# A graph-attention and adjacency kernel: the row of q by way of DRAM and one spreading load, with new order lists

## The chip, the cores and the metric

The kernel runs on one core of one Trainium2 chip. The metric is device time in microseconds (us): the median of several runs, beside one execution that the hardware profiler recorded. The engines are TensorE (PE in the profile, PEld for its weight loads), VectorE (DVE), ScalarE (ACT), GpSimd (POOL) and SyncE (SP), which only issues DMAs here.

## The reference

There are 32 batches x[b] of 512 channels by 1024 nodes, a matrix adj of 512 by 512, vectors wq, wk and bm of 512 and a bias of 1024. All is f32.

```
q, k   = wq . x, wk . x                                # one number per node
scores = leaky(q[n] + k[m], slope 0.01)                # 1024 x 1024
att    = softmax(scores over n)
agg    = x att^T;  gnn0 = relu(adj agg + bm)
x      = layernorm(x + gnn0, over the 1024 nodes)      # layer 0
x      = layernorm(x + (adj * adj)^T x + bias)         # layer 1, adj * adj elementwise
```

## The kernel before

The attention of layer 0 is never made as a matrix. exp(leaky(q + k)) is one product of exponentials where q + k > 0 and another where it is not, so if the nodes are sorted by q, the sum over n for a node m is a prefix sum plus a suffix sum at a place that depends on k[m]. A batch passes through these steps; the short name is the one that the order lists use:

- `ld` loads x[b] in four pieces of 0.5 MB (L87). `pa` (parts, L221) multiplies with wq and wk into one PSUM bank, the nodes in four groups of 256, group g at partition 32g (q) and 32g + 1 (k). `pc` (L229) copies that to SBUF on ScalarE, `co` (L236) transposes it, and `cc` (L241) copies q and k to `qkc`: node j*128 + p at partition p, column j.
- `ro` (row, L252) makes the row of q on all partitions: eight transposes of a column of q broadcast to 128, into a PSUM tile of 1024 floats. `rc` (row_copy, L261) copies it on VectorE to `qb` and takes its maximum in the same instruction; two small instructions make -max and -0.01 max (L262, L263).
- `rk` (L271, eight times, VectorE) counts for 128 nodes how many q are larger: their rank. `ct` (L284, eight times, ScalarE, a Sign with a sum) counts the same for -k. `re`, `oq` and `ce` turn these into indices and set bounds; `we` takes exponentials.
- `z` (product, L310, eight times) is adj times x for 128 nodes, 3.43 us of TensorE each; `zc` (L316, ScalarE) copies it to the one buffer `zt`. `sc` (scatter, L324, GpSimd, indirect DMA) writes the rows of zt to DRAM in the order of rank.
- `sl` loads the sorted rows to the one buffer `tab`, eight consecutive rows to a partition (L343), `se` takes exponentials (L348, L349), `u` and `d` (L362, L372, VectorE) sum along a partition upward and downward, `cu`, `cd` (L380, TensorE) and `uc`, `dc` (L387, ScalarE) carry over partitions, and `tu`, `te`, `td` (L405, L414) add the carries.
- `tw` and `tl` write the table of sums to DRAM (L422, 2 MB twice, and L425, one row). `g` (L432, eight indirect DMAs on GpSimd) gathers its rows into the one buffer `got`. `mw`, `ms`, `mx` (L445 to L459) mix the two halves, and `t` (turn, L482) transposes the mix.
- `r`, `s0`, `rt`, `rce`, `n0` (L490 to L508) add it to x and normalize: layer 0 is done.
- Layer 1 is one level of Strassen-Winograd on quarters: `t1` to `t4` (VectorE, L519 to L533) form differences; t1 overwrites a quarter of x, t2 has a tile of its own, t3 and t4 lie in zt. `U`, `V`, `Y`, `Z`, `11`, `12`, `21` (L540, L575, 1.7 us of TensorE each, twice) multiply, and U and Z begin with a small matmul for the bias (L538). `Uc`, `Vc`, `Zc`, `up`, `lr`, `ll`, `ls` take the results, `s1`, `r1`, `n` (L468, L475, L631) normalize, and `st` writes the output (L636).

TensorE sees in the steady state the end of layer 1 of one batch, four z of the next, transposes of the mix, parts and cols of the one after, and four more z.

The order on every engine is written out by hand: under a manual schedule each instruction is issued where it stands in the lists `head`, `loop` and `tail`, whose words are an operation, a batch (relative to the loop's in `loop`, to the last in `tail`) and an index. The program is laid out for every engine in this one order, and an engine takes its own instructions strictly in order; a wait therefore holds all that stands behind it on that engine. SP's DMAs are on one queue. Buffers are reused by tag; a tile waits for the readers of the one before it in that buffer. In the loop the words of interest stand thus (others left out):

```
t.-3.1 r.-3.1 pa.0 t.-3.0 pc.0 co.0 st.-4.2 z.-1.4 cc.0 z.-1.5 n.-4.3 st.-4.3 cd.-2 z.-1.6 dc.-2 td.-2.0
td.-3.1 ro.-1 tw.-3.0 z.-2.7 tw.-3.1 tl.-3 t1.-4 rc.-1 U.-4.0 rk.-1.7 U.-4.1 rk.-1.5 ct.-1.3 rk.-1.0 11.-4.1
```

(the second line is the start of the next turn of the loop, where batches are counted one lower).

Of the kernel before, what the change touches and what calls it, by code (L numbers as in the profile page):

```python
# [49 lines left out]
def adj_resnorm_kernel(  # L50
# [48 lines left out]
    nbm = const.tile([P, CT], F32, name="nbm")  # L99
# [21 lines left out]
    eps = const.tile([P, 1], F32, name="eps")  # L121
    nc.vector.memset(eps, EPS)
    power = const.tile([P, CT], F32, name="power")
# [12 lines left out]
    zero = one.tile([P, ZR], F32, tag="carry", name="zero")[0:1, :]  # L136
    nc.vector.memset(zero, 0.0)
    sorted_z = [dr.tile([N, ZR], F32, name=f"sorted_z_{i}") for i in range(2)]
# [3 lines left out]
    spare = const.tile([1, 1], F32, name="spare")  # L142
# [7 lines left out]
    first_0 = const.tile([6, P], BF16, name="first_0")  # L150
    first_10 = const.tile([6, P], BF16, name="first_10")
# [25 lines left out]
    def bias_parts(b):  # L177


        own = const.tile([6, 8], F32, name="own")  # L180
# [4 lines left out]
        nc.vector.tensor_copy(first_0, own[:, 4:5].broadcast_to([6, P]))  # L185
        nc.vector.memset(first_10, 1.0)
        rest, done = room[:, 0, :], room[:, 1, :]
        for i in range(3):
            part = one.tile([P, N], BF16, tag="junk_s", name=f"bias_part_{i}")[0:6, 0:H]
            nc.vector.tensor_copy(part, rest)  # L190
            if i < 2:
                nc.vector.tensor_tensor(rest, rest, part, ALU.subtract)
            if i == 0:
                nc.vector.tensor_scalar(done, part, own[:, 0:1], None, ALU.mult)
            else:
                nc.vector.scalar_tensor_tensor(
                    done, part, own[:, i : i + 1], done, ALU.mult, ALU.add
                )
# [27 lines left out]
    def parts_copy(b):  # L226
        s = st[b]
        s.part = one.tile([P, Q], F32, tag="part", name=f"part_{b}")
# [9 lines left out]
    def cols_copy(b):  # L238
        s = st[b]
        s.qk = s4.tile([P, NT, 2], F32, tag="qk", name=f"qkc_{b}")  # L240
# [5 lines left out]

    def row(b):

        s = st[b]
        s.ps = p2.tile([P, N], F32, tag="w", name=f"q_tp_{b}")  # L250
        for j in range(NT):
            nc.tensor.transpose(  # L252
                s.ps[:, j * P : (j + 1) * P], s.qk[:, j, 0:1].broadcast_to([P, P]), ident
            )

    def row_copy(b):
        s = st[b]
        s.qb = one.tile([P, N], F32, tag="qb", name=f"qb_{b}")
        top = s4.tile([P, 3], F32, tag="top", name=f"top_{b}")
        s.top, s.ntop = top[:, 0:1], top[:, 1:3]  # L260
        nc.vector.tensor_scalar(s.qb, s.ps, 1.0, None, ALU.mult, ALU.max, accum_out=s.top)  # L261
# [19 lines left out]
    def count(b, j):  # L281
        s = st[b]
        junk = one.tile([P, N], BF16, tag="junk_s", name=f"junk_s_{b}_{j}")
# [114 lines left out]
    def carry_down_copy(b):  # L398
        st[b].carry = one.tile([P, ZR], F32, tag="carry", name=f"carry_{b}")
# [62 lines left out]
    def stats(b, name):  # L462
        return [sp.tile([P, CT], F32, tag=t + name, name=f"{t}{name}_{b}") for t in ("tot", "var")]

    def spread(b, i, t, v, name):

        junk = one.tile([P, N], BF16, tag="junk_s", name=f"junk_{name}_{b}_{i}")
# [30 lines left out]
    def root0(b):  # L498
            v = st[b].v0
            nc.scalar.activation(v[1], v[1], AF.Sqrt, scale=1.0 / N**3, bias=eps)  # L500

    def root0_end(b):
            v = st[b].v0
            nc.vector.reciprocal(v[1], v[1])  # L504
    
# [39 lines left out]
    def rows1(b, m):  # L545
        s = st[b]
        if not s.v1:
            s.v1 = stats(b, "1")
            s.nb = sp.tile([P, CT], F32, tag="nb", name=f"nb_{b}")
            s.part2 = sp.tile([P, CT], F32, tag="part2", name=f"part2_{b}")  # L550
# [84 lines left out]
    def store(b, m):  # L635
# [7 lines left out]
        "rc": row_copy, "rk": rank, "re": rank_end, "ct": count, "ce": count_end,  # L643
# [21 lines left out]
    bias.0 ld.1 ld.2 ld.3 pa.0 z.0.0 pc.0 co.0 zc.0.0 z.0.1 cc.0 ro.0 zc.0.1 pa.1 rc.0 ct.0.1  # L665
    rk.0.1 z.0.2 ct.0.3 rk.0.7 pc.1 rk.0.2 ct.0.5 z.0.4 rk.0.3 ct.0.2 rk.0.4 ct.0.7 rk.0.6 z.0.6
    zc.0.4 zc.0.2 rk.0.0 rk.0.5 co.1 zc.0.6 z.0.5 re.0 cc.1 ct.0.4 oq.0 sc.0.1 sc.0.6 z.0.3
    sc.0.0 zc.0.5 ct.0.6 sc.0.5 sc.0.2 z.0.7 zc.0.3 sc.0.4 ct.0.0 sc.0.3 ro.1 zc.0.7 sc.0.7
    z.1.0 rc.1 rk.1.3 ct.1.6 ct.1.5 rk.1.1 z.1.6 sl.0.0 sl.0.1 rk.1.7 rk.1.5 z.1.2 zc.1.6 rk.1.6
    ct.1.4 rk.1.0 zc.1.0 se.0.0 oq.1 rk.1.2 z.1.4 se.0.1 u.0.0 ct.1.1 ce.0 u.0.1 u.0.2 z.1.1  # L670
    rk.1.4 u.0.3 u.0.4 z.1.5 u.0.5 zc.1.1 zc.1.4 u.0.6 ct.1.3 u.0.7 zc.1.2 ct.1.7 d.0.7 pa.3
    d.0.6 zc.1.5 re.1 d.0.5 sc.1.1 cu.0 pc.3 d.0.4 ct.1.2 sc.1.5 co.3 z.1.3 d.0.3 uc.0 sc.1.2
    cc.3 d.0.2 ct.1.0 tu.0.0 sc.1.0 sc.1.4 z.1.7 d.0.1 zc.1.3 te.0 sc.1.3 d.0.0 tl.0 tu.0.1
    sc.1.6 cd.0 ro.3 dc.0 zc.1.7 pa.2 td.0.0 sc.1.7 z.2.5 rc.3 tw.0.0 rk.3.0 ct.3.0 ct.3.6
    td.0.1 z.2.0 zc.2.5 ct.3.3 ce.1 tw.0.1 rk.3.6 pc.2 ct.3.1 co.2 z.2.4 rk.3.3 ct.3.2 rk.3.1
    ct.3.4 rk.3.4 ct.3.5 z.2.3 cc.2 rk.3.7 zc.2.0 ct.3.7 rk.3.5 g.0.0 sl.1.0 zc.2.4 sl.1.1 ro.2
    rk.3.2 g.0.3 z.2.6 rc.2 g.0.1 ct.2.4 rk.2.2 zc.2.3 z.2.7 rk.2.6 ct.2.0 rk.2.1 we.0 se.1.0
    ct.2.3 rk.2.5 z.2.1 g.0.2 u.1.0 ce.3 g.0.4 u.1.1 oq.2 u.1.2 g.0.6 se.1.1 zc.2.6 rk.2.0 z.2.2
    zc.2.7 g.0.5 ct.2.7 rk.2.3 g.0.7 mw.0.0 rk.2.4 z.3.0 ms.0.2 ms.0.1 mx.0.2 ms.0.0 rk.2.7
    zc.2.1 ms.0.3 ct.2.1 u.1.3 z.3.4 re.2 mx.0.0 sc.2.6 ct.2.2 mw.0.1 sc.2.5 mx.0.1 ms.0.6  # L680
# [282 lines left out]
```

## Time and profile before

| what | value |
|---|---|
| median of 3 runs | 2062.61 us (2061.65 to 2064.26) |
| the profiled execution's own time | 2065.32 us |
| its span, first to last instruction | 2063.6 us |
| mean granted TensorE clock | 0.991 |
| DMA traffic | 541.04 MB, 262 GB/s over the span |
| DMA busy share, SP's queue / GpSimd's queue | 41.2% / 26.0% of 16 engines |
| GpSimd busy | 874.6 us (42%) |

The page of a profile gives, for each engine, its busy time and share of the span. A group's line names the line of the code, the engine, the operation, output<-input by tile name, the shapes and the count; after the bar stand its busy time and the mean duration of one instruction in ns, and after a second bar the idle time of the engine just before such instructions, with what ended it. A stretch's line has its bounds and length, then busy time and count of each engine (PE, PEld, DVE, ACT, POOL), the granted clock, the share of time that the 16 DMA engines were busy, and GB/s. A line of the timeline has start, duration, engine, line, operation and how many were merged. A line of waits has the waiting engine with its tile and line, the releaser, the sum of the idle time, how often, and the longest.

### The profile page before, as it was taken

The numbers are of one execution on the slowest core, as the hardware profiler recorded it, in microseconds if no ns is written. First come the engines' busy times: TensorE is split into PE (matmuls) and PEld (weight loads), VectorE is DVE, ScalarE is ACT, GpSimd is POOL, SyncE is SP. The second block draws the span as 40 slices with busy tenths as digits, with TensorE's granted clock in tenths as the row PEclk, the third lists the DMA queues.
The fourth block names the chain that finished last, engine by engine and source line by source line (L and its number), as shares of the span: only waits on it lengthen the run. The fifth ranks groups of instructions, "written<-read, shape, count | busy, mean of one in ns | idle before, by whom it ended". The sixth has DMA issues, their size and how long they took to land. (4 is left out here: it accounts for less than half of the span.)

```text
span 2063.6 us, 22066 instructions
## 1 busy us (share of the span) xinstructions
PE 2004.7 (97%) x6609; PEld 956.7 (46%) x6609; DVE 1674.9 (81%) x2778; ACT 1496.3 (73%) x2560; POOL 874.6 (42%) x1106
## 2 busy tenths in 40 slices
PE   8999999999999999999999999999999999999976
PEld 4444444444444444444444544444444444444432
DVE  6888898798877889887889888789778888789672
ACT  3566787678776777777777777777777777767566
POOL 4344543344343444443444443453444443443421
PEclk9999999999999999999999999999999999999988
DMA  5558776866667766667766767766677766677752
GB/s 226 212 222 312 275 287 266 306 264 257 271 245 291 307 255 246 271 266 292 306 241 250 273 268 296 290 249 258 255 276 306 276 244 268 245 269 273 286 204 82
DMA packets 137967, 541.04 MB, mean 262 GB/s; under 512 B 14404, under 2 KB 14416, under 8 KB 129656
## 3 DMA queue, kind: packets, MB, share of 16 engines
q1 hardware_dynamic: 80464, 337.47, 41.2%
q0 software_dynamic: 57344, 202.15, 26.0%
q8 instruction: 52, 0.85, 0.2%
q14 instruction: 67, 0.55, 0.1%
q10 hardware_dynamic: 40, 0.02, 0.0%
HBM read 270.29 MB, written 269.29 MB: 261 GB/s over the span
## 5 line engine op out<-in xcount | busy, mean ns | idle before, releaser
L310 PE MATMUL z_ps<-adj_t,x 128*128 128x512 f32 x2048 | 906.6, 593 | 0.4 <-ACT zt L316 0.4
L310 PEld LDWEIGHTS z_ps<-adj_t,x 128*128 128x128 f32 x2048 | 384.1, 190 | 448.0 <-issue 439.5
L324 POOL DMA_INDIRECT sorted_z<-zt,to x256 | 377.2, 1473 | 481.0 <-ACT zt L316 403.7
L432 POOL DMA_INDIRECT got<-table,of x256 | 262.2, 1024 | 209.6 <-issue 87.8
L271 DVE SCALAR_TENSOR_TENSOR junk_v<-qb,qkc,tie 128x1024 uint8<-128x1024 f32 x256 | 328.2, 1282 | 4.0
L284 ACT ACTIVATE junk_s<-qb,qkc 128x1024 bf16<-128x1024 f32 x256 | 293.9, 1148 | 18.9 <-DVE qb L261 17.0
L475 POOL TENSOR_SCALAR var<-var 128x1 f32<-128x1 f32 x128 | 46.3, 362 | 461.9 <-ACT junk L468 458.6
L454 ACT ACTIVATE got<-got,w 128x512 f32<-128x512 f32 x256 | 172.2, 713 | 64.2 <-DVE w L449 56.6
L316 ACT COPY zt<-z_ps 128x512 f32<-128x512 f32 x256 | 144.4, 577 | 68.4 <-PE z_ps L310 63.2
L459 DVE SCALAR_TENSOR_TENSOR got<-got,w 128x512 f32<-128x512 f32 x256 | 180.9, 745 | 10.9 <-ACT got L454 10.7
L490 DVE SCALAR_TENSOR_TENSOR x<-agg_ps,nbm,x 128x1024 f32<-128x1024 f32 x128 | 161.4, 1280 | 23.1 <-PE agg_ps L482 22.7
L372 DVE SCALAR_TENSOR_TENSOR tab<-tab,ac 128x513 f32<-128x513 f32 x224 | 168.0, 750 | 3.0
L631 ACT ACTIVATE g<-g,nb,var 128x1024 f32<-128x1024 f32 x128 | 157.8, 1238 | 11.8 <-POOL nb L625 11.8
L468 ACT ACTIVATE junk<-g,tot 128x1024 bf16<-128x1024 f32 x128 | 146.6, 1146 | 21.3 <-DVE g L595 16.8
L362 DVE SCALAR_TENSOR_TENSOR tab<-tab,ac 128x514 f32<-128x514 f32 x192 | 144.5, 752 | 16.9 <-ACT ac L348 11.7
L468 ACT ACTIVATE junk<-x,tot 128x1024 bf16<-128x1024 f32 x128 | 146.8, 1147 | 13.6 <-DVE x L490 8.3
L405 DVE TENSOR_TENSOR tab<-tab,carry 128x2052 f32<-128x2052 f32 x64 | 144.8, 2292 | 11.5 <-ACT carry L387 11.5
L540 PE MATMUL sum_ps<-x,adj 128*128 128x512 f32 x256 | 131.4, 637 | 16.3 <-ACT x L508 16.3
L482 PE MATMUL agg_ps<-ident,got 128*128 128x128 f32 x1024 | 133.4, 278 | 11.2 <-issue 4.7
L508 ACT ACTIVATE x<-x,var 128x1024 f32<-128x1024 f32 x128 | 138.5, 1149 | 0.7 <-DVE var L504 0.6
L601 DVE SCALAR_TENSOR_TENSOR g<-sum_ps,g 128x512 f32<-128x512 f32 x64 | 44.0, 687 | 111.8 <-ACT junk_s L284 75.3
L482 PEld LDWEIGHTS agg_ps<-ident,got 128*128 128x128 f32 x1024 | 115.2, 143 | 36.3 <-DVE x L490 12.2
(121 smaller groups left out, 2698.8 us busy)
## 6 DMA issues: line engine op xcount, KB each, us to landing
table<-tab SPq DMA_DIRECT2D x64, 2056.0 KB
tab<-sorted_z SPq DMA_DIRECT2D x64, 1028.0 KB
x<-in_x_dram SPq DMA_DIRECT2D x128, 512.0 KB
out_dram<-g SPq DMA_DIRECT2D x128, 512.0 KB
sorted_z<-zt,to POOLq DMA_INDIRECT x256
got<-table,of POOLq DMA_INDIRECT x256
adj_in<-in_adj_dram SPq DMA_DIRECT2D x1, 1024.0 KB
table<-end SPq DMA_DIRECT2D x32, 2.0 KB
```

The lines of the kernel that those rows point to most:

```text
L271: nc.vector.scalar_tensor_tensor(junk, s.qb, s.q[:, j : j + 1], tie[:, at : at + N], ALU.subtract, ALU.is_gt, accum_out=s.rank[:, j : j + 1],)
L284: nc.scalar.activation(junk, s.qb, AF.Sign, bias=s.k[:, j : j + 1], accum_out=s.sign[:, j : j + 1])
L310: nc.tensor.matmul(s.z[j], xt[:, c, j * P : (j + 1) * P], adj_t[:, c, :], start=(c == 0), stop=(c == CT - 1),)
L324: nc.gpsimd.indirect_dma_start(out=sorted_z[b % 2][:, :], out_offset=bass.IndirectOffsetOnAxis(ap=s.to[:, j : j + 1], axis=0), in_=zt[:, j ...
L372: nc.vector.scalar_tensor_tensor(v, v, c, s.zs[:, j + 1, 0:D], ALU.mult, ALU.add)
L432: nc.gpsimd.indirect_dma_start(out=s.got[:, j, :], out_offset=None, in_=table[b % 2][:, :], in_offset=bass.IndirectOffsetOnAxis(ap=s.of[:, ...
L454: nc.scalar.activation(down, down, AF.Copy, scale=s.w[:, 1, j : j + 1])
L459: nc.vector.scalar_tensor_tensor(up, up, s.w[:, 0, j : j + 1], down, ALU.mult, ALU.add)
L468: nc.scalar.activation(junk, t, AF.Square, bias=v[0][:, i : i + 1], scale=-float(N), accum_out=v[1][:, i : i + 1],)
L482: nc.tensor.transpose(s.agg[o][:, j * P : (j + 1) * P], s.got[:, j, o * P : (o + 1) * P], ident)
L490: nc.vector.scalar_tensor_tensor(t[:, o, :], s.agg[o], nbm[:, o : o + 1], t[:, o, :], ALU.max, ALU.add, accum_out=s.v0[0][:, o : o + 1],)
L631: nc.scalar.activation(g, g, AF.Identity, bias=s.nb[:, m : m + 1], scale=s.v1[1][:, m : m + 1])
```

## The change

The row of q no longer passes through TensorE. `pc` copies the parts to SBUF as before; a new step `qw` (row_out) writes the q partitions (0, 32, 64, 96) of `part` as a row of 1024 floats to DRAM, and `ro` is now one DMA on SP that loads this row to all 128 partitions of `qb`. `rc` (row_max) only takes the maximum. There are two buffers of qb instead of one. To find room, `part`, the downward carry and T2 share one buffer, ScalarE's unused results ("junk_s") are written in 8 bits instead of 16, qkc has three buffers instead of four, the two bias selectors are one column each and broadcast, and several small tiles are put together. All three order lists are new, with qw after pc and with rc later than before; their description says that they were laid out for 5 per cent longer work on the engines beside TensorE. The loop now covers batches 13 to B - 6 instead of 12 to B - 7.

```diff
-    first_0 = const.tile([6, P], BF16, name="first_0")
-    first_10 = const.tile([6, P], BF16, name="first_10")
+    first = const.tile([6, 16], BF16, name="first")
+    first_0, first_10 = first[:, 0:1].broadcast_to([6, P]), first[:, 1:2].broadcast_to([6, P])
...
     def parts_copy(b):
         s = st[b]
-        s.part = one.tile([P, Q], F32, tag="part", name=f"part_{b}")
+        s.part = one.tile([P, 2, H], F32, tag="T2", name=f"part_{b}")[:, 0, 0:Q]
         nc.scalar.copy(s.part, s.ps)
...
-        s.qk = s4.tile([P, NT, 2], F32, tag="qk", name=f"qkc_{b}")
+        s.qk = s3.tile([P, NT, 2], F32, tag="qk", name=f"qkc_{b}")
...
+    def row_out(b):
+        rows = q_row[b % 2].rearrange("(g o c) -> g o c", g=CT, o=1)
+        nc.sync.dma_start(
+            out=rows, in_=st[b].part.rearrange("(g r) c -> g r c", g=CT)[:, 0:1, :]
+        )
+
     def row(b):
 
         s = st[b]
-        s.ps = p2.tile([P, N], F32, tag="w", name=f"q_tp_{b}")
-        for j in range(NT):
-            nc.tensor.transpose(
-                s.ps[:, j * P : (j + 1) * P], s.qk[:, j, 0:1].broadcast_to([P, P]), ident
-            )
-
-    def row_copy(b):
-        s = st[b]
-        s.qb = one.tile([P, N], F32, tag="qb", name=f"qb_{b}")
+        s.qb = sp.tile([P, N], F32, tag="qb", name=f"qb_{b}")
+        nc.sync.dma_start(out=s.qb, in_=q_row[b % 2].partition_broadcast(P))
+
+    def row_max(b):
+        s = st[b]
         top = s4.tile([P, 3], F32, tag="top", name=f"top_{b}")
         s.top, s.ntop = top[:, 0:1], top[:, 1:3]
-        nc.vector.tensor_scalar(s.qb, s.ps, 1.0, None, ALU.mult, ALU.max, accum_out=s.top)
+        nc.vector.tensor_reduce(s.top, s.qb, axis=AX.X, op=ALU.max)
...
-        junk = one.tile([P, N], BF16, tag="junk_s", name=f"junk_s_{b}_{j}")
+        junk = one.tile([P, N], U8, tag="junk_s", name=f"junk_s_{b}_{j}")
...
-        st[b].carry = one.tile([P, ZR], F32, tag="carry", name=f"carry_{b}")
+        st[b].carry = one.tile([P, 2, H], F32, tag="T2", name=f"carry_{b}").rearrange("p i c -> p (i c)")[:, 0:ZR]
...
-        return [sp.tile([P, CT], F32, tag=t + name, name=f"{t}{name}_{b}") for t in ("tot", "var")]
+        t = sp.tile([P, 2, CT], F32, tag="tv" + name, name=f"tv{name}_{b}")
+        return [t[:, 0, :], t[:, 1, :]]
...
-        junk = one.tile([P, N], BF16, tag="junk_s", name=f"junk_{name}_{b}_{i}")
+        junk = one.tile([P, N], U8, tag="junk_s", name=f"junk_{name}_{b}_{i}")
...
-    for b in range(12, B - 6):
+    for b in range(13, B - 5):
```

The new loop list, from the transposes of the mix to the first products of layer 1, and the start of the head:

```
t.-3.1 uc.-2 n.-4.0 t.-3.3 r.-3.1 s1.-4.3 pa.0 st.-4.0 d.-2.3 s0.-3.1 r.-3.3 r1.-4.3 t.-3.0 pc.0 d.-2.2 s0.-3.3 qw.0
t.-3.2 d.-2.1 co.0 n.-4.2 sc.-1.2 z.-1.4 r.-3.2 st.-4.2 sc.-1.3 r.-3.0 st.-4.1 s0.-3.2 cc.0 s0.-3.0 d.-2.0 z.-1.5
tu.-2.0 zc.-1.4 rt.-3 sc.-1.4 te.-2 tu.-2.1 n.-4.3 cd.-2 st.-4.3 z.-1.7 ro.0 dc.-2 rce.-3 tl.-2 zc.-1.5 td.-2.0 n0.-3.0
sc.-1.5 n0.-3.2 td.-2.1 z.-1.6 tw.-2.0 n0.-3.1 n0.-3.3 rc.0 tw.-2.1 U.-3.0 rk.0.5 ct.0.4 zc.-1.6 rk.0.2 U.-3.1 ct.0.1
rk.0.0 11.-3.1 Uc.-3.1 t1.-3 Uc.-3.0 zc.-1.7 rk.0.7 ct.0.5 11.-3.0 sc.-1.7 t2.-3 ct.0.2 sc.-1.6 Z.-3.0 rk.0.1 g.-2.0
...
ld.1 bias.0 pa.0 z.0.0 pc.0 qw.0 ro.0 pa.1 ld.2 zc.0.0 co.0 z.0.5 cc.0 pc.1 qw.1 rc.0 ct.0.7 rk.0.3
```

## The prediction

> **What bounds the kernel now.** I read the page's busy line first, then busy time by stretch, then TensorE's own waits, and last the timeline of one batch in the middle.
>
> ```profile
> PE 2004.7 (97%) x6609; PEld 956.7 (46%) x6609; DVE 1674.9 (81%) x2778; ACT 1496.3 (73%) x2560; POOL 874.6 (42%) x1106
> ```
>
> TensorE (PE) is at work in all but 58.9 us of the span. Where that idle time lies is shown by the busy time of five stretches:
>
> ```profile
> 7.00:100.00 93.00, 91.37 (x363) 44.44 (x364) 72.52 (x121) 45.91 (x86) 37.52 (x48) 1.00 0.55 212
> 100.00:300.00 200.00, 192.97 (x611) 91.41 (x610) 172.86 (x290) 143.23 (x255) 94.38 (x111) 0.99 0.73 278
> 300.00:1900.00 1600.00, 1593.24 (x5287) 761.23 (x5286) 1331.23 (x2210) 1200.37 (x2054) 693.28 (x867) 1.00 0.70 272
> 1900.00:2063.60 163.60, 127.08 (x352) 59.53 (x350) 95.65 (x153) 105.47 (x169) 45.98 (x72) 0.90 0.47 181
> ```
>
> The first pair of numbers is length and PE busy time. From 300 to 1900 us PE is idle 6.8 us of 1600; the gaps are in the fill (7.0 us before the first matmul, 8.7 us up to 300) and in the drain (36.5 us). So in the middle a batch costs what PE needs for it, and the drain is a chain of latencies. TensorE's waits between 60 and 1900 us, in all 12.9 us, are short ones for neighbours:
>
> ```profile
> PE agg_ps L482 <- DVE got L459: 4.5, 9, 1.0
> PE qk_tp L236 <- ACT part L229: 4.0, 3, 3.2
> ```
>
> The work that goes is the group "q_tp", and the timeline shows what it occupies:
>
> ```profile
> L252 PE MATMUL q_tp<-ident,qkc 128*128 128x128 f32 x256 | 33.3, 273 | 0.5 <-DVE qkc L241 0.5
> ...
> 990.48 3.59 PE L310 MATMUL z_ps<-adj_t,x 128*128 128x512 f32 x8
> 993.91 1.04 PE L252 MATMUL q_tp<-ident,qkc 128*128 128x128 f32 x8
> 994.78 3.60 PE L310 MATMUL z_ps<-adj_t,x 128*128 128x512 f32 x8
> 998.31 0.39 PE L538 MATMUL sum_ps<-bias_p,first 6*128 6x512 bf16 x1
> ```
>
> The product after it starts 0.87 us after the transposes start, not 1.04: the ends overlap. The next q_tp starts at 1055.91, so a batch takes 62.0 us.
>
> **What the Trainium skill says.** (1) "Perfetto Trace Analysis", Identifying the Most-Contended Engine: matmul busy time misleads, since matmuls are pipelined. The trace agrees: the group's 33.3 us of busy time is only 32 slots of 0.87 to 0.88 us. (2) "DMA: Bandwidth & Descriptors", Two DMAs through the same engine are not ordered: a DMA that reads what another wrote must be held at its issuing engine until the first one's semaphore is full. So the row load stands on SP until the row write has landed; the kernel before has the same with its sorted rows. (3) The same page, Anatomy of one DMA, puts about 2 us of fixed cost on each DMA. Here it is more: in the drain half a load of sorted rows (1 MB) was issued at 1937.24 and used at 1942.89, 5.6 us, of which 2.5 us are bytes at the 421 GB/s that the fullest 5 us moved; 3.1 us stay. (4) "VectorE: DVE Perf Modes", the perf-mode tier table: tensor_reduce has only the 1x rate. No large one is in this trace.
>
> **The change, part by part.**
>
> *Transposes removed.* 32 slots of 0.88 us are 28.2 us; the waits for "qkc" ahead of them were 0.5 us more. All lie where PE never rests or before the last product (about 1931 us), on which the drain hangs, so the whole 28.7 us leave the path. Bounds: 27.8 (0.87 each) to 33.3 (the group's busy time).
>
> *VectorE.* The fused copy from PSUM (1219 ns and 83 to read the sum) becomes a reduction of 1024 floats in SBUF. An estimate from the page's 1x rate at 0.96 GHz is 1.07 us and a start; the 1024-wide tensor-tensor rows take 1.22 us. I take 1.22, bounds 1.07 to 1.35. It is hidden: VectorE is idle about 10 us of each 62. Uncovered, the upper bound would cost 0.05 us a batch, 1.6 us in all.
>
> *Two DMAs a batch on SP.* The row write is small and on few partitions; the nearest row, "table<-end", keeps SP 1.11 us. The row load is 128 rows of 4 KB, 0.5 MB, 0.35 us of SP. The traffic per batch goes from 16.9 to 17.4 MB. Where the load goes the engines are half free:
>
> ```profile
> 1049.00:1051.00 2.00, 2.00 (x6) 0.95 (x5) 2.00 (x3) 2.00 (x4) 1.74 (x3) 1.00 0.20 80
> 1051.00:1053.00 2.00, 2.00 (x8) 1.23 (x7) 1.19 (x2) 1.97 (x4) 1.99 (x2) 1.00 0.63 240
> 1053.00:1055.00 2.00, 2.00 (x6) 0.86 (x5) 1.64 (x2) 2.00 (x5) 0.85 (x1) 1.00 0.56 218
> 1055.00:1057.00 2.00, 2.00 (x12) 1.39 (x11) 2.00 (x2) 2.00 (x3) 1.64 (x2) 1.00 0.31 132
> ```
>
> (the last two columns are DMA share and GB/s). The question is whether the row lands in time. Count from the first agg transpose of the batch, T (1038.91 in the trace). In the new loop list SP has, in order, qw, three stores, ro, tl, tw. The write waits for the copy of qk_ps, about T+3, and lands by T+9 even at the 4.85 us that a loaded "table<-end" took. The last store waits for n.-4.3, whose place among ScalarE's work is nearly the old one (T+12.4), so ro is issued at T+13.1. With 5.6 us, as above (half the bytes, but one 0.5 MB store just ahead), the row is there at T+18.7. VectorE, going through the same r, d, tu and td steps, is free at T+19.7 (T+19.0 in the trace plus one d moved behind T, 0.7). Then rc 1.4, three ranks 4.0 and T1 1.22 end at T+26.3. PE needs T1 at Z: agg transposes, parts and cols 5.6, four z 13.7, cd 0.9, two U 4.5, two C11 3.4, thus T+28.3. So 2 us of room, and the row may land as late as T+21.7, 8.6 us after issue, before PE feels it. On ScalarE count, zc, sc and then the gathers queue behind the row: at T+18.7 plus 5 us of ACT work the scatters go at T+24 and the gathers at T+27, where the old ones began at T+31.5. tl and tw stand behind ro on SP, but tw waits for td until T+17 anyway; 0.5 MB ahead of it is 1.2 us of the 4.5 us thus won. Cost taken: nothing; bounds 0 to 3 us a batch (below).
>
> *Sharing of buffers.* part and carry now lie in T2's buffer. The carry copy waits for qw, landed at T+9 against cd at T+13; part waits for V of the batch before, 20 us earlier. Cost 0; if the write were 4 us later, ScalarE would stand and td with it. A second qb buffer lets the load start while the old row is still read.
>
> *8-bit junk on ScalarE.* Results in bf16 take 1146 to 1148 ns and in f32 1149 (L508): the type does not show. VectorE's 8-bit result costs nothing either (1282 against 1280). I take 0; at most 0.1 us for 16 a batch, 1.6 us, in 15 us of ScalarE idle time. No gain: the elements stay.
>
> *Broadcast bias weights.* Four weight loads of 91 ns a batch, against 137 for the broadcast f32 ones of q_tp; if 46 ns each came out uncovered, 6 us. They run beside matmuls: 0. Less is not possible, as many columns are loaded. Merged small tiles: set-up and the same readers, 0.
>
> *New lists.* Room beside PE should take away part of the 12.9 us of short waits; bounds 0 to 12.9, I take 3. What is late next is then PE itself. In the fill, the first row passes DRAM behind the second batch's load: 5 MB at 326 GB/s end near 17 us, the row lands near 23, and VectorE had its first copy done at 23.9; 0, bounds -2 to +3. In the drain the order of PE is nearly the old one (one C21 is moved into a gap, but the last mix ends only 0.3 us before it); 0, bounds -2 to +4.
>
> Sum against the profiled execution: span 2063.6 - 28.7 - 3.0 = 2031.9, and with the 1.7 that lie around the span (2065.32 in all) 2033.6. That execution was 2.7 above the median of the runs, 2062.61: I predict 2062.6 - 31.7 = 2030.9, say **2031**. Per batch: 62.0 becomes 61.1.
>
> **Rivals.**
> - *A, as summed*, 2031, 2022 to 2040. For it: PE has no idle time in the middle, and the slot is measured directly.
> - *B, the row is a little late in part of the batches* (PE stalls 0.5 us in 28): 2031 + 14 = 2045. For it: only 2 us of room. Against: half-free DMA queues.
> - *C, slower: the wait for the row takes the place of the transposes.* In the saturated stretch 1075 to 1090 the first half of the sorted rows, issued at 1072.14, was used only at 1083.69: 11.5 us. At that price the row lands at T+24.6, 2.9 us past the limit; rc holds VectorE, T1 behind it, and Z on PE, in 28 batches: 81 us, so 2031 + 81 = 2112. It turns slower once PE's stall passes 31.7/28 = 1.1 us, a landing later than 9.7 us after issue.
> - *D, nothing comes of it:* another loop holds 62 us (tab: load, sums, spread, write; VectorE at 83%), or fill and drain give the gain back: 2062. Against: VectorE has 10 us free, and the tab loop waits too.
>
> **How the numbers follow.** Chances: A 0.74, B 0.12, C 0.08, D 0.06. The range reaches from A with most waits gone, 2022, into B, 2047, and leaves out C, D and B's far end. 0.2% (4 us) is about what a measurement of this kernel can tell from no change. Faster: A, B and 0.01 of D, 0.87; same 0.04; slower: C and 0.01 of D, 0.09.
>
> **What would show it.** The line q_tp gone; z to z 3.43 us where a slot lay; a period near 61.1 us; PE idle still some 7 us from 300 to 1900; a wait of VectorE for qb under 1 us a batch; ScalarE's counts and squares still near 1147 ns. Wrong would be: PE waiting at Z (L540, pair_ps) for VectorE's T1, waits of VectorE's reduction for the load of qb above 2 us, or a drain longer than 37 us of PE idle time.

## The result and the profile after

The changed kernel takes **2053.53 us** (median of 12 runs, 2050.18 to 2061.18) against 2062.9 us before (12 runs beside it, 2061.58 to 2066.96): ratio 0.9962, 95% interval 0.9952 to 0.9973. The predicted 2031 us and the range from 2022 us miss it: 9 us were gained where 32 were expected. Eight of the twelve runs took 2050.2 to 2054.6 us and four 2059.3 to 2061.2; the profiled execution, 2050.36 us with a span of 2048.6 us (15.0 us less than before's 2063.6), is one of the eight.

The busy line of the page and the busy time by stretch (columns as ahead of the prediction):

```profile
PE 1978.8 (97%) x6353; PEld 931.7 (45%) x6353; DVE 1671.6 (82%) x2746; ACT 1491.4 (73%) x2560; POOL 864.3 (42%) x1114
```

```profile
7.00:100.00 93.00, 93.00 (x343) 43.76 (x344) 75.27 (x122) 44.69 (x86) 39.19 (x49) 1.00 0.67 250
100.00:300.00 200.00, 184.80 (x576) 87.12 (x575) 167.72 (x279) 142.31 (x250) 88.89 (x109) 0.97 0.72 277
300.00:1900.00 1600.00, 1592.03 (x5132) 752.00 (x5131) 1345.67 (x2211) 1212.71 (x2086) 686.97 (x879) 1.00 0.72 281
1900.00:2048.60 148.60, 108.92 (x307) 48.68 (x305) 80.28 (x128) 90.43 (x140) 45.76 (x71) 0.91 0.51 193
```

TensorE's busy time fell by 25.9 us. The slots of the transposes were 28.2 us; the 2.3 us between fit work at a reduced clock (0.97 instead of 0.99 between 100 and 300 us). But TensorE is idle 69.8 us instead of 58.9: 15.2 us instead of 7.0 between 100 and 300 us, 39.7 instead of 36.5 in the drain, 8.0 instead of 6.8 in between (all of it before 600 and after 1700 us), and 1.6 us less before 100 us. So 10.9 us of the 25.9 came back as waiting.

In the loop the transposes went as predicted. The timeline of TensorE in the middle shows the sixteen records of two z in one piece where the slot of q_tp lay, the group "q_tp" is gone from the page, and from 620 to 1700 us no wait of TensorE is left:

```profile
986.51 1.03 PE L381 MATMUL carry_ps_False<-tab,behind 128*128 128x257 f32 x4
987.38 7.03 PE L311 MATMUL z_ps<-adj_t,x 128*128 128x512 f32 x16
994.34 0.39 PE L540 MATMUL sum_ps<-bias_p,first 6*128 6x512 bf16 x1
```

From the first U of one batch to that of the next it is 1055.58 to 1116.61, 61.03 us, where 61.1 was predicted. Counted over the program by the start of `pa` of a batch (us; the rows below the second belong to experiments told further down):

| kernel | batch 4 | 5 | 6 | 7 | 8 | 10 | 11 | 31 | span's end |
|---|---|---|---|---|---|---|---|---|---|
| before | 171.0 | 245.3 | 305.6 | 355.9 | 419.0 | 543.3 | 605.2 | 1852.2 | 2063.6 |
| after | 168.2 | 238.5 | 305.1 | 357.4 | 420.5 | 547.7 | 609.1 | 1834.4 | 2048.6 |
| after, a second profile | 166.4 | 236.8 | 303.8 | 356.2 | 425.0 | 550.6 | 613.4 | 1838.1 | 2051.5 |
| new lists, row by transposes | 170.6 | 242.0 | 310.1 | 362.6 | 425.7 | 553.1 | 615.2 | 1866.3 | 2083.3 |
| old lists, DRAM row | 174.0 | 252.8 | 316.0 | 374.9 | 439.7 | 564.5 | 625.9 | 1848.7 | 2061.7 |
| old head with transposes, DRAM row from batch 11, second profile | 170.3 | 245.0 | 304.8 | 356.8 | 420.5 | 546.4 | 608.3 | 1830.1 | 2041.7 |
| the same, no C12 in batches 0 to 10 | 172.1 | 247.9 | 311.0 | 362.8 | 425.9 | 550.7 | 612.3 | 1834.6 | 2045.1 |

The twenty batches from 11 to 31 take 1225.3 us instead of 1247.0, 21.7 less. The drain after batch 31's start takes 214.2 instead of 211.4. And batch 11 begins 3.9 us **later** than before, though eleven batches of transposes, 9.7 us, are gone ahead of it. Up to batch 5 the changed kernel leads by 6.8 us; it loses 6.2 of them between batches 5 and 6 and 4.3 between 9 and 10. The longest waits of TensorE between 7 and 620 us of the changed kernel are these:

```profile
PE qk_tp L235 <- ACT part L228: 7.8, 2, 4.6
...
PE carry_ps_True L381 <- ACT zt L317: 2.9, 1, 2.9
PE sum_ps L542 <- DVE zt L531: 2.5, 1, 2.5
PE sum_ps L542 <- DVE g L603: 2.3, 2, 1.5
```

The columns are the sum, how often, and the longest. The 4.6 us lie at 246, the 2.5 at 288, the 2.9 at 544 us; the last line's are near 400 us. The other wait of the first line, 3.2 us at 173 us, has its like before (3.2 us at 180 us). Of the one at 246 us the timeline of four engines tells the chain:

```profile
236.85 0.26 POOL L627 TENSOR_SCALAR nb<-tv 128x1 f32<-128x1 f32 x1
...
238.76 4.50 DVE L406 TENSOR_TENSOR tab<-tab,carry 128x2052 f32<-128x2052 f32 x2 [0.23 <-ACT carry L388]
...
239.19 4.12 POOL L627 TENSOR_SCALAR nb<-tv 128x1 f32<-128x1 f32 x1
...
243.34 1.24 ACT L633 ACTIVATE g<-g,nb,tv 128x1024 f32<-128x1024 f32 x1 [2.93 <-POOL nb L627]
...
245.62 0.35 ACT L228 COPY part<-qk_ps 128x256 f32<-128x256 f32 x1
...
246.03 0.69 PE L235 MATMUL qk_tp<-ident,part 128*128 128x128 f32 x2 [4.57 <-ACT part L228]
```

GpSimd's instruction for the bias of the normalization took 4.12 us instead of 0.26: it ran beside VectorE's two large additions of carries and ended at 243.31, 0.05 us after them (243.26). ScalarE's normalization waited 2.93 us for it; the copy of the q/k parts stands behind that in the new head list; TensorE waited 4.57 us for the copy. The Trainium skill, "SBUF — State Buffer", SBUF: two separate sides, says that VectorE and GpSimd share a port pair that an operation of VectorE with two SBUF inputs locks for its whole length; the trace agrees, and six more of GpSimd's small instructions end within 0.15 us after such an addition, having taken 1.5 to 2.1 us.

### The profile page after: what moved, and what is told of

It is laid out like the page before. It is cut to its first block, busy times and chain, and to the rows that moved or that the text cites. A ratio compares the mean times of both kernels' runs of the same rounds, so it can differ in the third digit from the quotient of the medians.

```text
span 2048.6 us, 21657 instructions
## 1 busy us (share of the span) xinstructions
PE 1978.8 (97%) x6353; PEld 931.7 (45%) x6353; DVE 1671.6 (82%) x2746; ACT 1491.4 (73%) x2560; POOL 864.3 (42%) x1114
## 5 line engine op out<-in xcount | busy, mean ns | idle before, releaser
L325 POOL DMA_INDIRECT sorted_z<-zt,to x256 | 354.7, 1386 | 450.6 <-ACT zt L317 379.1
L433 POOL DMA_INDIRECT got<-table,of x256 | 278.7, 1089 | 227.1 <-issue 77.7
L285 ACT ACTIVATE junk_s<-qb,qkc 128x1024 uint8<-128x1024 f32 x256 | 294.4, 1150 | 11.4 <-DVE of L292 5.4
L477 POOL TENSOR_SCALAR tv<-tv 128x1 f32<-128x1 f32 x128 | 41.9, 328 | 469.7 <-ACT junk L470 466.4
L492 DVE SCALAR_TENSOR_TENSOR x<-agg_ps,small,x 128x1024 f32<-128x1024 f32 x128 | 161.6, 1280 | 18.4 <-PE agg_ps L484 18.0
L597 DVE SCALAR_TENSOR_TENSOR g<-pair_ps,g 128x1024 f32<-128x1024 f32 x64 | 78.2, 1221 | 106.3 <-PE pair_ps L542 100.6
L633 ACT ACTIVATE g<-g,nb,tv 128x1024 f32<-128x1024 f32 x128 | 157.6, 1238 | 5.8 <-POOL nb L627 5.8
L470 ACT ACTIVATE junk<-g,tv 128x1024 uint8<-128x1024 f32 x128 | 146.7, 1146 | 20.7 <-DVE g L597 18.0
L470 ACT ACTIVATE junk<-x,tv 128x1024 uint8<-128x1024 f32 x128 | 147.1, 1149 | 15.6 <-DVE x L492 12.8
L510 ACT ACTIVATE x<-x,tv 128x1024 f32<-128x1024 f32 x128 | 138.3, 1148 | 1.7 <-DVE tv L506 1.7
```

The source lines that it names most:

```text
L285: nc.scalar.activation(junk, s.qb, AF.Sign, bias=s.k[:, j : j + 1], accum_out=s.sign[:, j : j + 1])
L325: nc.gpsimd.indirect_dma_start(out=sorted_z[b % 2][:, :], out_offset=bass.IndirectOffsetOnAxis(ap=s.to[:, j : j + 1], axis=0), in_=zt[:, j ...
L433: nc.gpsimd.indirect_dma_start(out=s.got[:, j, :], out_offset=None, in_=table[b % 2][:, :], in_offset=bass.IndirectOffsetOnAxis(ap=s.of[:, ...
L470: nc.scalar.activation(junk, t, AF.Square, bias=v[0][:, i : i + 1], scale=-float(N), accum_out=v[1][:, i : i + 1],)
```

## The experiments

**The start list, or the row's traffic?** Theory L said that the new start list loses the gain; its rival T, that the row's 0.5 MB a batch delay the gathers, whose results VectorE waits for at "mw" (96.2 us in 48 waits after, 51.1 us in 25 before). Four kernels test it.

*The lists of before, the row by way of DRAM* (`qw` behind `pc`, `ro` behind SP's next DMA, the q/k parts in a buffer of their own; the first change is shown against before, the second against the changed kernel):

```diff
-    bias.0 ld.1 ld.2 ld.3 pa.0 z.0.0 pc.0 co.0 zc.0.0 z.0.1 cc.0 ro.0 zc.0.1
+    bias.0 ld.1 pa.0 z.0.0 pc.0 qw.0 ro.0 ld.2 ld.3 co.0 zc.0.0 z.0.1 cc.0 zc.0.1
...
-    for b in range(13, B - 5):
+    for b in range(12, B - 6):
```

> The changed program with the three order lists of before: only a qw after each pc is put in, ro is moved from its old place to just after the next DMA that SP issues, the loads of batches 2 and 3 stand behind the first row, and part has its own buffer again (the old order would not let it lie in T2's). Theory L (the fill of the new lists is what ate the gain): the old fill and drain are back and each batch is a slot shorter, so about 2062.9 - 28 = 2035. Theory T (the row's half megabyte a batch and its place on the DMA queue delay the gathers and so stall TensorE): the traffic is the same as in the changed kernel, so no better than 2050.

Measured: 2058.98 us, ratio 0.9972 (0.9962 to 0.9982). L missed by 24 us, and T's number (no better than 2050) held. The loop is as fast as with the new lists (61.1 us a batch), but batch 11 begins at 625.9 us. VectorE's waits from 7 to 620 us show what is new there:

```profile
DVE top L262 <- DMA qb<-q_row: 24.9, 6, 8.6
```

In the old start list `rc` stands close behind `cc`; the row needs longer than the transposes did, and VectorE waits 24.9 us for it in six batches. L in this form falls: the row by way of DRAM needs an `rc` that stands later in the start. That these waits make all of the 20.7 us is not shown.

*The new lists, the row by transposes again*, issued on TensorE where rc stands:

```diff
-        nc.sync.dma_start(out=s.qb, in_=q_row[b % 2].partition_broadcast(P))
...
-        nc.vector.tensor_reduce(s.top, s.qb, axis=AX.X, op=ALU.max)
+        for j in range(NT):
+            nc.tensor.transpose(s.row[:, j * P : (j + 1) * P],
+                s.qk[:, j, 0:1].broadcast_to([P, P]), ident)
+        nc.vector.tensor_scalar(s.qb, s.row, 1.0, None, ALU.mult, ALU.max, accum_out=s.top)
```

> The new lists, but the row is made by eight transposes and the fused copy again (at ro's place in the lists where q is already in SBUF, else at rc's), with no row write and no row load. L: the new lists keep their fill, and 28 us of slots come back: 2053.5 + 28 = about 2081, slower than before. T: with the traffic gone the stalls go too, and it is about 2062, as before, or less.

Measured: 2086.69 us, ratio 1.0106 (1.0092 to 1.0121); L hit. Against the changed kernel's 2053.5 the row by DRAM is worth 33 us under these lists, but with transposes these lists (and the small edits, which this kernel keeps) cost 21 us against before. In the start they cost 10.0 us (615.2 against 605.2 at batch 11), and TensorE's timeline shows the changed kernel's three waits again, to 0.01 us, without any DMA of the row:

```profile
249.51 0.69 PE L235 MATMUL qk_tp<-ident,part 128*128 128x128 f32 x2 [4.56 <-ACT part L228]
...
292.70 5.37 PE L545 MATMUL sum_ps<-zt,S 128*128 128x512 f32 x8 [2.55 <-DVE zt L534]
```

```profile
550.70 0.70 PE L384 MATMUL carry_ps_True<-end,before 128*128 128x257 f32 x2 [2.92 <-ACT zt L320]
```

So these waits belong to the new start list, not to the row's traffic. VectorE waits here for the transposes too, which stand where the list has `rc` (27.4 us in nine waits up to 620 us), but TensorE's waits above 1 us in the start are all ones that the changed kernel also has. And the waits at "mw", on which T rests, are in the new lists without the traffic (before, after, this kernel):

```profile
DVE w L445 <- DMA got<-table,of: 51.1, 25, 8.7
DVE w L446 <- DMA got<-table,of: 96.2, 48, 6.1
DVE w L449 <- DMA got<-table,of: 95.4, 48, 6.8
```

*The changed kernel with less traffic:*

```diff
-        nc.sync.dma_start(out=out[b, m * P : (m + 1) * P, :], in_=st[b].g[m])
+        n = 8 if m == 3 else N
+        nc.sync.dma_start(out=out[b, m * P : (m + 1) * P, 0:n], in_=st[b].g[m][:, 0:n])
```

> The changed kernel, with the store of the last 128 channels of each batch cut to 8 columns, so a batch moves half a megabyte less, which is what the row load added; most of a quarter of the output is left unwritten. L: same as the changed kernel, 2053 within 3. T: some 10 us come back, 2043 or less, and the waits of the mix weights for the gathers fall from 96 us towards the 51 us of before.

Measured: 2051.33 us, ratio 0.9932 (0.9918 to 0.9947), waits for gathers 89.4 us in 42. Taking out as much traffic as the row added brings about 2 us of the 22 that are missing (T said 2043 us or less): L's number, and T is at most a small part.

*The changed kernel once more:*

> The changed kernel once more, unaltered: times between 2050 and 2061 as in its twelve runs, and a second profile. L: the stalls ahead of about 550 us come again at the same places with nearly the same lengths. T: they move about with the gathers.

Measured: 2053.43 us, ratio 0.9944 (0.9932 to 0.9957). The waits at 246, 288 and 544 us come again; a wait of 5.5 us near 404 us, 1.5 in the first profile, brings batch 11 to 613.4 us. The kernel's own start varies by some 4 us.

**Can the waits be taken out?** The first kernel moves two words of the head list, the second and the third one more each; a fourth puts the start of before ahead of a loop with the DRAM row. Here theory F is that the start eats the gain stall by stall, theory D that the traffic does.

```diff
-    s0.2.3 n.1.2 td.3.1 pa.5 s1.1.3 st.1.2 t.2.1 r.2.0 r1.1.3 pc.5 s0.2.2 qw.5 co.5 z.5.0
+    s0.2.3 td.3.1 pa.5 s1.1.3 t.2.1 r.2.0 r1.1.3 pc.5 s0.2.2 qw.5 co.5 n.1.2 st.1.2 z.5.0
```

> The changed kernel with two words of the start list moved: the normalising and the storing of row block 2 of batch 1 come behind the q/k copy and the column matmuls of batch 5 instead of ahead of them. Theory F (the fill's order eats the gain, stall by stall): the TensorE stall of 4.57 us near 246 us goes, and the slowed clock behind it, so 5 to 7 us less than the changed kernel, about 2047 us. Theory D (the row's 0.5 MB broadcast keeps the DMA engines busy and delays the gathers; the stalls are only where the lateness shows): the stall turns up elsewhere and the time stays within 2 us of the changed kernel, 2052 to 2055.

Measured: 2056.9 us, ratio 0.9964 (0.9949 to 0.9978).

```diff
-    r1.2.1 mw.3.1 Vc.2.0 ms.3.2 up.2.0 ms.3.5 ms.3.4 mx.3.5 ms.3.7 t3.2 zc.5.4
+    r1.2.1 t3.2 mw.3.1 Vc.2.0 ms.3.2 up.2.0 ms.3.5 ms.3.4 mx.3.5 ms.3.7 zc.5.4
```

> As the kernel with the two words moved, and the third difference of batch 2 (T3) moved on VectorE ahead of the second mix weights of batch 3, so that it doesn't stand behind work that waits for gathers. Theory F: the stall of 2.55 us near 288 us goes as well, with the clock behind it, 3 to 4 us more off, about 2043 us. Theory D: still 2052 to 2055.

Measured: 2056.63 us, ratio 0.9967 (0.9955 to 0.9978).

```diff
-    zc.9.0 ll.6.1 re.9 mw.7.1 ms.7.2
+    zc.9.0 ll.6.1 zc.9.2 re.9 mw.7.1 ms.7.2
...
-    s1.6.2 d.8.6 mx.7.5 zc.9.2 mx.7.6
+    s1.6.2 d.8.6 mx.7.5 mx.7.6
```

> As the kernel before it in this list, and one copy of the product (row block 2 of batch 9) moved on ScalarE ahead of the mixing that waits for the gathers of batch 7. Theory F: the stall of 2.92 us near 544 us goes as well, 3 to 4 us more off, about 2039 us. Theory D: 2052 to 2055.

Measured: 2055.2 us, ratio 0.9954 (0.9939 to 0.997). F's numbers missed by 10 to 16 us; D's 2052 to 2055 us are nearer. The waits did go or shrink (4.57 to 2.31 us at 244; those at 288 and 544 us gone in the third), but others came: "g" 2.0 us at 278, 1.7 at 292, and this one on TensorE at 404 us,

```profile
403.76 3.78 PE L542 MATMUL sum_ps<-zt,adj 128*128 128x512 f32 x4 [5.17 <-DVE g L603]
```

which hangs on ScalarE's exponentials, which wait for the sorted rows:

```profile
402.27 0.30 ACT L349 ACTIVATE ac<-tab,top 128x4 f32<-128x4 f32 x1 [7.00 <-DMA tab<-sorted_z]
```

In the changed kernel's first profile the same load landed in time:

```profile
399.05 0.30 ACT L349 ACTIVATE ac<-tab,top 128x4 f32<-128x4 f32 x1 [3.36 <-DMA tab<-sorted_z]
```

There SP issued it at 390.70, just ahead of GpSimd's second gather (390.92); in the kernel with three words moved at 391.06, just behind it (390.50), and it was used 3.2 us later. In the nine traces with the new start list this load stands ahead of that gather in three, and is used 6.2 to 8.4 us after its issue; behind it in six, 10.1 to 11.5 us after its issue in five and 7.8 in the one with less to store. The first and the second profile of the unaltered kernel differ in just this, so the list does not settle it; no run moved that order alone. A stall taken out of the start was no gain here: the next one came.

*The head list of before with transposes in batches 0 to 10, the DRAM row from batch 11 on, in the loop and tail lists of before:*

```diff
+        if b < LAST_TP:
+            s.row = p2.tile([P, N], F32, tag="w", name=f"q_tp_{b}")
+            for j in range(NT):
+                nc.tensor.transpose(
+                    s.row[:, j * P : (j + 1) * P], s.qk[:, j, 0:1].broadcast_to([P, P]), ident
+                )
+            return
         s.qb = sp.tile([P, N], F32, tag="qb", name=f"qb_{b}")
         nc.sync.dma_start(out=s.qb, in_=q_row[b % 2].partition_broadcast(P))
```

> The order lists of before, with the row by transposes in batches 0 to 10 exactly where before has them, and by DRAM and one spreading load from batch 11 on. Theory F: batch 11 starts at about 605 us as in before, the 20 batches after it take about 1223 us as in the other kernels with the DRAM row, and the end 213 us: a span of about 2041 and a time of about 2043 us. Theory D: the loop with its broadcasts on the old lists shows no more than the 4 us of gain that the old lists with the DRAM row showed, about 2058 us.

Measured: 2043.99 us, ratio 0.9909 (0.9894 to 0.9924), span 2041.9. F hit to 1 us, in part by luck: batch 11 began at 608.5 where about 605 was expected, and the drain took 209.8 where 213 was. The twenty batches between took 1223.6 (1223 expected): the loop's gain is real and carries to the end when the start list is left alone. This is the best order that the runs found: 19.3 us below before beside it, where the changed kernel had 9.4 and 12.2.

**Is TensorE the bound of the start at all?** The prediction took that for granted. Theory P says yes; theory Q, that what TensorE saves there turns into waits. In batches 0 to 10 one of the two matmuls of each C12 is left out, with no new DMA and no new order. This was meant to free as much as the transposes, 0.9 us a batch, but it frees twice that. One 128x512 matmul of the code is two records in the trace: a z, four matmuls, is eight records in 3.43 us, so a matmul is 0.86 us and not 0.45. The cut takes 1.7 us a batch, 18.9 us in all, and 13.7 of them before batch 11 starts, since only batches 0 to 7 have come to their C12 by then.

```diff
     def C12(b, g):
+        if b < 11:
+            nc.tensor.matmul(
+                st[b].pair[g][:, H:N], S4[:, 1, g * P : (g + 1) * P], quarters(b)[3][:, 1, :],
+                start=False, stop=True, skip_group_check=True,
+            )
+            return
         quarter(st[b].pair[g][:, H:N], S4, quarters(b)[3], g)
```

> The kernel with the start list of before, transposes in batches 0 to 10 and the DRAM row after them, less TensorE work in the start: in batches 0 to 10 the last product of each upper block (C12) takes one of its two 128x512 matmuls, so half of that product is missing from the output there. That is 2 matmuls of 0.45 us in the flow, 0.90 us a batch, as much as the eight transposes, with no DMA added and no order changed. Theory P (the start is bound by TensorE like the loop): 11 times 0.9, so 10 us less than the same kernel with all matmuls, 2034 us. Theory Q (the start is bound by the chain of copies, ranks, DMAs and mixing beside TensorE; what TensorE saves there turns into waits): 2041 to 2044 us.

Measured: 2050.99 us, ratio 0.9926 (0.9906 to 0.9947). P's 10 us less, 19 by the true size of the cut, did not come; Q's 2041 to 2044 us was missed as well, by 7 us. Batch 11 starts at 618.0 us, 10 us later than with all matmuls.

The same on the changed kernel:

> The changed kernel with the same matmuls left out: in batches 0 to 10 one of the two of each C12 product, 0.90 us a batch, half of that product missing from the output there. Theory P: about 10 us less than the changed kernel, 2043 us. Theory Q: 2050 to 2054 us, with longer waits on TensorE between 100 and 600 us instead.

Measured: 2047.72 us, ratio 0.9915 (0.9899 to 0.9931). That is 16.4 us below before beside it, where the changed kernel had 9.4 and 12.2: 4 to 7 of the 18.9 us came through, between both theories. Batch 11 starts at 607.9 us.

The third kernel has the old head, all matmuls, and the DRAM row from batch 7 on:

```diff
-    LAST_TP = 11
+    LAST_TP = 7
```

> As the kernel with the start list of before and the DRAM row from batch 11 on, but with the DRAM row from batch 7 on. The old lists with the DRAM row everywhere lost their 17 us before batch 7 begins and none after it. Theory P: batches 7 to 10 gain 0.9 us each, 2040 us. Theory Q: those four gain nothing, 2044 us.

Measured: 2043.81 us, ratio 0.9895 (0.9876 to 0.9914), with batch 11 at 607.5 us, 0.9 us earlier where P's four slots make 3.5. This is Q's number.

**Is it VectorE, or the DMAs?** VectorE is busy 86 to 90 per cent between 160 and 300 us. Its mixing is halved in batches 0 to 10 (theory V; W: neither), or less is stored there.

```diff
+        if b < 11:
+            up, down = up[:, 0 : C // 2], down[:, 0 : C // 2]
         nc.vector.scalar_tensor_tensor(up, up, s.w[:, 0, j : j + 1], down, ALU.mult, ALU.add)
...
+        n = 8 if b < 11 and m > 1 else N
```

> The kernel with the start list of before and the DRAM row from batch 11 on, with VectorE's mixing of batches 0 to 10 done on half of its columns (half of the weighted sum is missing from the output there): 8 times about 0.27 us, 2.1 us a batch less on VectorE, nothing else changed. Theory V (VectorE's queue, 86 to 90 per cent busy between 160 and 300 us against 82 to 84 in the loop, makes TensorE wait in the start): TensorE's 9 us of waits between 100 and 600 us shrink to a third, 2038 us. Theory W (DMA landings and the fixed order make the waits): 2042 to 2046 us.

Measured: 2043.19 us, ratio 0.99 (0.9886 to 0.9914). This is W's number.

> As above, and one matmul of 0.45 us of each C12 product left out too in batches 0 to 10 (half of that product is missing). Theory V: the TensorE work saved shows now, 10 us less than without the TensorE cut, 2030 to 2034 us. Theory W: 2045 to 2051 us, as with the TensorE cut alone.

Measured: 2044.42 us, ratio 0.9904 (0.9889 to 0.9918), about W; V missed by 10 us or more.

> The changed kernel with VectorE's mixing of batches 0 to 10 done on half of its columns (half of the weighted sum is missing from the output there). Theory V: most of the 20 us of TensorE's waits between 100 and 600 us go, about 2040 us. Theory W: 2049 to 2054 us.

Measured: 2051.12 us, ratio 0.9939 (0.9927 to 0.9951). W's number again.

> The kernel with the start list of before, the DRAM row from batch 11 on and the TensorE cut in batches 0 to 10 (half of each C12 product missing), and of row blocks 2 and 3 of those batches only 8 columns stored (the rest of these blocks is left unwritten): 1 MB a batch less DMA traffic. If the DMA traffic sets the pace of the start: the TensorE cut shows, 2034 us. If not: 2045 to 2051 us.

Measured: 2045.71 us, ratio 0.9911 (0.9891 to 0.9931): the TensorE cut stays hidden, so these DMAs alone are not the bound either. Each of the two cuts takes away what the TensorE cut had cost (2051 us), but nothing more.

**A double dose, side by side.** The whole C12 is left out in batches 0 to 10, beside the same kernel with all matmuls. That is 3.4 us a batch, 37.8 us in all and 27.5 before batch 11 starts, where 1.8 us a batch and 20 in all were meant.

```diff
     def C12(b, g):
+        if b < 11:
+            return
         quarter(st[b].pair[g][:, H:N], S4, quarters(b)[3], g)
```

> The kernel with the start list of before and the DRAM row from batch 11 on, once more, as the measure for the next one: 2042 to 2046 us.

Measured: 2044.62 us, ratio 0.9904 (0.989 to 0.9918).

> The same with the whole C12 product left out in batches 0 to 10 (it is missing from the output there): 4 matmuls of 0.45 us, 1.8 us a batch and 20 us in all less for TensorE. Theory P (TensorE sets the pace of the start): 2024 us. Theory Q (it does not): no more than 4 us below the kernel with all matmuls, 2040 to 2052 us, with the first 12 batches as long as before and TensorE's waits longer by about 20 us.

Measured: 2048.88 us, ratio 0.9928 (0.9915 to 0.9941). Some 38 us less work on TensorE, and 4 us more time. The busy lines show 88 records fewer, those of 44 matmuls (first the kernel with all of them):

```profile
PE 1983.3 (97%) x6441; PEld 939.7 (46%) x6441; DVE 1677.1 (82%) x2757; ACT 1496.2 (73%) x2560; POOL 873.7 (43%) x1106
PE 1961.0 (96%) x6353; PEld 926.0 (45%) x6353; DVE 1675.8 (82%) x2757; ACT 1494.2 (73%) x2560; POOL 869.6 (43%) x1106
```

The stretches of the kernel with all matmuls, then those of the kernel without C12 in the start:

```profile
7.00:100.00 93.00, 91.83 (x362) 44.66 (x363) 72.82 (x122) 46.00 (x87) 37.95 (x48) 1.00 0.55 213
100.00:300.00 200.00, 192.72 (x614) 92.19 (x613) 173.53 (x290) 143.57 (x255) 95.98 (x111) 0.99 0.73 279
300.00:620.00 320.00, 314.93 (x1076) 150.70 (x1075) 264.56 (x436) 242.29 (x411) 132.01 (x166) 1.00 0.68 265
```

```profile
7.00:100.00 93.00, 92.04 (x364) 44.86 (x365) 72.68 (x122) 46.08 (x87) 37.91 (x48) 1.00 0.55 213
100.00:300.00 200.00, 182.63 (x562) 84.53 (x561) 167.19 (x279) 137.65 (x245) 95.18 (x108) 0.97 0.72 274
300.00:620.00 320.00, 305.36 (x1052) 145.74 (x1051) 265.71 (x445) 242.88 (x416) 131.25 (x168) 0.99 0.68 267
```

Where the time goes is plainer if TensorE is counted from 7 us up to each kernel's own start of batch 11 (us):

| kernel | matmul records | busy | idle | batch 11 starts |
|---|---|---|---|---|
| before | 1979 | 587.9 | 10.3 | 605.2 |
| new lists, row by transposes | 1979 | 591.0 | 17.2 | 615.2 |
| after | 1891 | 581.9 | 20.3 | 609.1 |
| after, a second profile | 1891 | 583.1 | 23.3 | 613.4 |
| old head, all matmuls | 1979 | 587.8 | 13.5 | 608.3 |
| old head, half of C12 | 1947 | 586.4 | 24.7 | 618.0 |
| old head, no C12 | 1915 | 572.3 | 33.0 | 612.3 |

Without C12, 64 records of 0.43 us are gone, 27.5 us, but busy time falls by 15.5 only: the work that stays takes 12.0 us longer, at a granted clock that falls to 0.97 between 100 and 300 us. Waiting grows by 19.5. Together batch 11 starts 4.0 us later. The waits come from everywhere (TensorE's waits from 7 to 620 us without C12; L618 adds the result of the lower right block on VectorE, L468 is the mixing on ScalarE, L575 the copy of U, L483 the squares):

```profile
PE sum_ps L555 <- DVE g L618: 8.5, 5, 3.1
...
PE sum_ps L555 <- ACT got L468: 3.8, 1, 3.8
PE sum_ps L555 <- ACT g L575: 3.4, 3, 1.2
PE sum_ps L555 <- ACT junk L483: 2.8, 1, 2.8
```

So TensorE, busy 98 per cent in the start, does not set its pace alone: work taken from it there came back as waits and as slower work. But this cut does not tell the start from the loop. The C12 of batches 8 to 10 come after batch 11 starts, where TensorE has next to no gaps, and there the cut brought little too. The four batches from 11 to 15 took 245.0 us without these C12 and 244.3 with them, though 10.3 us of work were gone; with half of them it was 242.3, of 5.2 us taken. Much depends, then, on which work is taken and how much at once. The transposes, 0.88 us a batch in the loop, came off in full there.

## Why the prediction missed

- **The step that failed** is the start, batches 0 to 10, in two terms of the sum. 10.2 us less were expected there (11 slots and the 0.5 us of waits for qkc); batch 11 came 3.9 us late, 14.1 us off.
  - *New lists: "In the fill ... 0, bounds -2 to +3"*, in place of which 10.0 us were measured (615.2 against 605.2, both with transposes): 6.9 us more of waiting on TensorE and 3.1 us more for the same matmuls, at a lower clock. The prediction looked only at the first row's landing, and that was right: the third q/k product starts at 63.9 us, before at 67.0. The order of the 600 us after it was not looked at. Up to 3.2 of the 10.0 us may be the small edits or the start's own variation, since the old head with these edits (but a buffer of its own for the parts) starts batch 11 at 608.3 to 608.5 us.
  - *Transposes: "the whole 28.7 us leave the path"*, since PE never rests. Under the new lists the eleven slots gave 6.1 us (615.2 to 609.1) where 9.7 were expected, and by the second profile 1.8; under the old head four of them gave 0.9 of 3.5. That TensorE was almost without gaps there was read as its being the bound.
- **In the loop the transposes were right.** Slots of 0.88 us; for the twenty batches from 11 to 31, 17.6 us of slots and 3.0 of waits were expected, and 21.7 came.
- **Drain.** 0.9 us less with its last slot was expected, 2.8 more came, 3.7 off and inside the bounds. The tail of before with the DRAM row took 208.8 to 213.0 us in its nine profiles, the new tail with it 213.4 to 217.5 in eight, so most of this is the new tail's order; TensorE's largest wait there is the same work as before (the normalized x, L508 before; 16.3 us before):

```profile
PE sum_ps L542 <- ACT x L510: 16.2, 3, 11.6
```

- The three sum up: 14.1 in the start (10.0 of the lists and 4.1 of the transposes), 3.7 in the drain, less 1.1 more gained in the loop, are the 16.7 us between the 31.7 predicted and the span's 15.0. Between the medians 9.4 us are left of the 15.0: the profiled execution of after lies 3.2 us below its median (its start is the better of the two seen), that of before 2.4 us above.
- **Row in time: right.** Where T is 973.91, ro was issued at 987.19 (T+13.3; T+13.1 predicted) and VectorE came to its maximum at T+18.5 without a wait. (The parts listed for PE's way to Z make T+28.1, not T+28.3, and the fullest 5 us of the trace before moved 451 GB/s, not 421; nothing hung on either.) In the whole program VectorE waited this much for the row:

```profile
DVE top L262 <- DMA qb<-q_row: 6.5, 5, 2.4
```

  Rival C's mechanism is the one that the old start list shows (24.9 us), but not in the loop. Of the signs of being wrong, two came: a wait above 2 us for the row, twice and only in the start, and 39.7 us of idle time in the drain where 37 was the mark.
- **VectorE's reduction: right.** 1212 ns, 1.22 taken. "VectorE: DVE Perf Modes" of the Trainium skill gives tensor_reduce the 1x rate only. As an estimate from it, 1024 elements at the page's 0.96 GHz are 1067 ns; the trace agrees, with 145 ns beside them.
- **8-bit junk: right.** 1150 and 1146 to 1149 ns.
- **Rival D was half right**, with the wrong sentence first: no other loop holds 62 us; start and drain gave much of the gain back. I gave it 0.06, since all I asked of the start was whether TensorE had gaps.

What sets the pace of the start is **not settled**. It is not TensorE alone, not VectorE's mixing alone (2.1 us a batch), not 1 MB of stores a batch alone. That it is the fixed order itself, with many chains of nearly the same length, fits all runs but was not shown by itself.

## What to carry to other kernels

A TensorE that is 98 per cent busy in a stretch need not set its pace alone: where the order is fixed and other chains are nearly as long, time taken from it turns into waits, and into slower work behind them. A run that leaves out some of its work asks this before a new mechanism is built, but size the cut by the records in the trace, and make the same cut in the loop, where the answer is known, before reading it in the start. Judge a pipeline's start, loop and drain apart, by the start times of one step in every batch, and don't multiply the loop's gain by the number of all batches. A new order list has a price of its own, to be measured with the old mechanism in it; here the best kernel kept the old start and took the new row only where it paid.

## What the runs showed of the hardware

- GpSimd's small instruction beside VectorE's f32 additions of two SBUF tiles: 4.12 us instead of 0.26, ended 0.05 us after them.
- Waits of TensorE cost more than their length, but not always. After the 2.55 us at 288 us eight records of 128x512 took 5.37 us instead of 3.60 (granted clock 0.76 from 286 to 293 us), after the 4.57 us at 246 us 24 took 12.48 instead of some 10.5 (0.53 from 244 to 251). After 3.23 us at 173 us sixteen took 7.03, the full rate (1.00 from 171 to 178); in the second profile of the same kernel, after 3.19 us at the same place, they took 8.36 (0.79 from 170 to 178). "TensorE: Matmul & The Clock Gate", HAM oscillation, of the Trainium skill warns of gaps above about 3.4 us; here shorter ones were enough, and one of nearly that length was not.
- One f32 128x512 matmul of the code is two records in the trace (1024 matmuls of z, 2048 records) and holds TensorE for 0.86 us in a flow.
- A load that was issued 0.36 us later, and so behind instead of ahead of one gather, was used 3.2 us later. Nine traces agree with an effect of that order, but for one with less to store; which of the two comes first changes from run to run of the same kernel.
